# The last part of a convolution and attention kernel: other units ahead of the last stage, x's half of the fusion first, output stores on ScalarE's queue, a one-image unit last

## The chip, the cores and the metric

One core of one Trainium2 chip runs the kernel. The metric is the device time of one execution in microseconds; the figure for a kernel is the median of its runs. One further execution was recorded by the hardware profiler; its span and its own time are given below. Engines are named as the profile names them: PE multiplies matrices (PEld is its weight load), ACT is the scalar engine, DVE the vector engine, POOL GpSimd, SP the sync engine; ACTq, SPq and POOLq are rows of DMA issues of these engines.

## The reference

Two images of 256 channels and 64 x 64 pixels go through two layers.

Layer 0 is attention over all pixels, fused with its input:

```python
q = proj(Wq, bq) / math.sqrt(hd); k = proj(Wk, bk); v = proj(Wv, bv)     # 8 heads of 32
attn = softmax(einsum('bnd,bmd->bnm', q, k))                             # 4096 x 4096 a head
fuse = einsum('bnm,bmd->bnd', attn, v)
hybrid = conv1x1(concatenate([x, fuse], axis=1), Wf, bf)
x = hybrid * m + x * (1.0 - m)
```

Layer 1 is a channel gate, attention inside windows of 8 x 8 pixels, and a gate out of two grouped convolutions:

```python
x = x * sigmoid(relu(xp @ ca_w1 + ca_b1) @ ca_w2 + ca_b2)
o = softmax(q k / sqrt(64)) v                  # 4 heads in each of 64 windows, then @ out_w
x = shuffle(x + o)                             # channels in 4 groups
y = relu(bn1(conv7x7(x, sa_w1, groups=64)))
y = bn2(conv7x7(y, sa_w2, groups=64))
return x * sigmoid(y)
```

All is in float32. The convolutions need rows of the whole image with a border of three, so a channel's convolution can begin only when every part of that image has been through layer 1's attention.

## The kernel before, in words

**Main loop.** `pipeline` walks through 1024 slots: two images b, eight chunks c of 512 pixels, two groups g of four heads, 32 blocks m of 128 keys. Each slot makes scores on PE (L580), exponentials on ACT (L590), the product with v on PE (L609) and the running sum of the exponentials on DVE (L611). `products` also registers, by `at(delay, action)`, what follows the last block of a chunk: the sums of the exponentials (`denominators`, L632), their reciprocal, two spreads of it over channels (`spread`, L647, with a copy on ACT) and the product that makes `f` (L664). A counter `now` runs with the slots, and an action is done when its delay has passed.

**Stage.** After each chunk a generator `stage(b, c)` is put in the queue `stages`. Between its `yield`s it records the fusion of x and f (eight matmuls, L677; x is kept in `xw`, and the first two of four products for an output half are of x, the others of f), the channel gate (L706, L714, a second small matmul and a tanh, L729), the projections of the windows' attention (L748, L761), scores, exponentials, v, a transpose, the product (L876, L887), the output projection (L898, L906), the sum (L909), and four stores (L924) of the result to `xs` in DRAM, two on SP and two on POOL. In the main loop a stage goes on by one step every four slots. After the last slot comes the stage of the last chunk of image 1, with no attention work left beside it: this is where the change lies.

**Convolutions.** `convolve` is another generator. Its work is cut into `items`: a unit `u` is 4 of the 64 convolution groups (16 channels), for image 0, image 1 or both. The two 7 x 7 convolutions are matmuls with banded weights, read as `w_s[u]` (896 KB, L959). For an item, x is read from DRAM (`load_x`, L966, 420 KB an image), the first convolution is 56 matmuls (L987) with a relu on ACT (L995), the second 56 matmuls (L1011) with two tanh (L1021) and a scaling copy (L1027) on ACT, the gate product on DVE (L1033), and 12 stores an image to the output (L1039), of which SP issues half and POOL half. The recorded order is: first convolution of item k+1, second convolution of item k, gate and stores of item k, loads. The first convolution has one PSUM buffer, the second three pairs, and the output tile `z` two buffers.

`items` lists 9 units of image 0, then the same 9 of image 1, then 7 units of both images: 25 items. Units of image 0 can run while the last chunk of image 1 is still in its stage, and fill its waits: after the last slot the loop below records, by turns, a step of the stage and a step of `convolve`. `now` goes on by 2 a turn.

```python
while later or stages:
    now[0] += 2
    run_later()
    run_stages()
    if later or stages:
        next(conv)
staged.append(True)
```

Only after `staged` is set may x of image 1 be loaded, since the last stage writes it. The four early x tiles `xea` come from before; later x tiles `xla` take over buffers of the attention.

**What sets the order.** The order of instructions on each engine is the order of recording, and each engine goes through its own list in order. A DMA that an engine issues stands in that list, too. An instruction waits on semaphores of what it depends on. DMAs of SP and ACT report their end in eight shared completion counters in turn, and a DMA waits until the one before it on its counter has landed.

Of the kernel before, what the change touches and what calls it, by code (L numbers as in the profile page):

```python
# [10 lines left out]
F32 = mybir.dt.float32  # L11
# [6 lines left out]
B, C, H, W = 2, 256, 64, 64  # L18
N = H * W
P = 128  # L20
KC = C // P
CH = 512
# [3 lines left out]
HG = 4  # L26
# [2 lines left out]
NPIECE = NMB // PB  # L29
AHEAD = 2  # L30
EB = 8
EARLY = 1 + EB
HEADS1, HD1 = 4, 64
WS = 8
NW = W // WS
# [2 lines left out]
WP = W + 2 * PAD  # L38
# [5 lines left out]
UG = 4  # L44
UQ = UG // 4
NU = NG // UG
# [8 lines left out]
def conv_seq_kernel(ctx: ExitStack, tc: tile.TileContext, a, out):  # L55
    nc = tc.nc
# [129 lines left out]
    with (  # L186
# [9 lines left out]
        for n in ("bq", "bk"):  # L196
            t = w0.tile([P, KC], F32, name=n)
            for g in range(KC):
                for j in range(HG):
                    h = HG * g + j  # L200
# [209 lines left out]
    def spread(row, n):  # L410
        f = row.shape[-1]
        return row.rearrange("p u f -> u p f").to_broadcast([NU, n, f])
# [58 lines left out]
    def pipeline(arm, shifted, pools):  # L471
# [25 lines left out]
        def at(delay, action):  # L497
            later.append((now[0] + delay, action))
# [99 lines left out]
        def products(i):  # L598
            b, c, g, m = slots[i]
            if m == 0:  # L600
                acc[0] = avp.tile([P, CH], F32, tag="av", name=f"av{arm}_{i}")
                acc[1] = ep.tile([P, HG, CH], F32, tag="sum", name=f"sum{arm}_{i}", bufs=3)
                totals[b, c, g] = acc[1]
            av, total = acc[0], acc[1]
            e, v = es[i], vts[b, c, g, m // PB]
            start, stop = m == 0, m == NMB - 1
            for j in range(HG):
                r = slice(32 * j, 32 * j + 32)
                nc.tensor.matmul(av[r, :], v[:, m % PB, r], e[:, j, :], start=start, stop=stop)  # L609
            if m > 0:  # L610
                nc.vector.tensor_add(total, first[0] if m == 1 else total, e)  # L611
            e = es.pop(i)
            if start:
                first[0] = e
            if stop:
                if g == 0:
                    fts[b, c] = fp.tile([P, KC, CH], F32, tag="f", name=f"f{arm}_{b}_{c}")
                f = fts[b, c]
                nc.scalar.copy(f[:, g, :], av)  # L619
                if g == 0:  # L620
                    return
                both = [totals.pop((b, c, gg)) for gg in range(KC)]
                inv = fp.tile([P, P], F32, tag="inv", name=f"inv{arm}_{i}")
                rd = fp.tile([P, KC, 4, P], F32, tag="rd", name=f"rd{arm}_{i}")


                def denominators():
                    s = psum2(f"dn{arm}_{i}")
                    for h in range(HEADS0):
                        for q in range(4):  # L630
                            r = slice(32 * q, 32 * q + 32)
                            nc.tensor.matmul(  # L632
                                s[r, 0, 0:P],
                                keysum[:, h].rearrange("p i h -> p (i h)"),
                                both[h // HG][:, h % HG, q * P : (q + 1) * P],
                                start=(h == 0),
                                stop=(h == HEADS0 - 1),
                            )
                    nc.scalar.copy(inv, s[:, 0, 0:P])


                def spread(hh):
                    t = psum2(f"rd{arm}_{i}_{hh}")
                    for gg in range(KC):
                        for q in range(2):
                            r = slice(64 * hh + 32 * q, 64 * hh + 32 * q + 32)
                            nc.tensor.matmul(  # L647
                                t[:, q, gg * P : gg * P + P],
                                spread_h[r, gg].rearrange("p j d -> p (j d)"),
                                inv[r, :],  # L650
                                start=True,
                                stop=True,
                            )
                    nc.scalar.copy(
                        rd[:, :, 2 * hh : 2 * hh + 2, :],
                        t[:, :, 0 : KC * P].rearrange("p q (g n) -> p g q n", g=KC),
                    )


                at(8, denominators)  # L660
                at(9, lambda: nc.vector.reciprocal(inv, inv))
                at(10, lambda: spread(0))
                at(11, lambda: spread(1))
                at(12, lambda: nc.vector.tensor_mul(f, f, rd.rearrange("p g q n -> p g (q n)")))  # L664


        def stage(b, c):
# [4 lines left out]
            t = gp.tile([P, KC, CH], F32, tag="t", name=f"t{tag}")  # L672
            x1 = gp.tile([P, KC, CH], F32, tag="x1", name=f"x1{tag}")
            xw = [x[:, kc, :].rearrange("p (r w c) -> p w r c", r=WS, w=NW) for kc in range(KC)]
            for oc in range(KC):
                for kc in range(2 * KC):
                    nc.tensor.matmul(  # L677
                        s[:, oc, :],
                        wf[:, kc, oc * P : (oc + 1) * P],
                        xw[kc] if kc < KC else f[:, kc - KC, :],  # L680
                        start=(kc == 0),
                        stop=(kc == 2 * KC - 1),
                    )
            for oc in range(KC):
                nc.scalar.activation(  # L685
                    t[:, oc, :], s[:, oc, :], AF.Identity, bias=bf[:, oc : oc + 1]
# [9 lines left out]
            nxt = (b, c + 1) if c + 1 < NCHUNK else (b + 1, 0)  # L696
            if nxt[0] < B:
                load_x(*nxt)
            yield

            half = CH // 2
            toks = [slice(half * h, half * h + half) for h in range(2)]
# [33 lines left out]

            u = wp.tile([P, KC, CH], F32, tag="u", name=f"u{tag}")
            nc.vector.scalar_tensor_tensor(u, t, 1.0, x1, ALU.add, ALU.mult)  # L738
            yield

            qks, es_, mxs, sums = [], [], [], []

# [72 lines left out]
                nc.vector.tensor_mul(e, e, rs.unsqueeze(2).to_broadcast([P, 8, 64]))  # L815

            project_out(0, project(0))
            yield
            window_scores(0)
            yield  # L820

            s = project(1)
            window_exp(0)
            project_out(1, s)
            yield
            window_scores(1)
            normalise(0)
            yield
# [34 lines left out]
                                )  # L863
            pt = wp.tile([P, 2, 2, KC, 2, 64], F32, tag="pt", name=f"pt{tag}")
            nc.scalar.copy(pt, st)
            yield

            s = psum2(f"o{tag}")
            o = s.rearrange("p w (a t q) -> p w a t q", a=KC, t=4)
# [14 lines left out]
            for kc in range(KC):  # L884
# [5 lines left out]
                    AF.Identity,  # L890
                    bias=bqkv[:, 4 + kc : 5 + kc],
                )
            yield
            s = psum2(f"op{tag}")
            y = gp.tile([P, KC, CH], F32, tag="t", name=f"y{tag}")
            for oc in range(KC):
# [32 lines left out]

        items = [(u, (b,)) for b in range(B) for u in range(EARLY)]
        items += [(u, tuple(range(B))) for u in range(EARLY, NU)]
        staged = []

        def convolve():
# [34 lines left out]
            def load_rows(k):  # L971

                while len(xs) < min(k + 1, len(items)) and (
                    staged or B - 1 not in items[len(xs)][1]
                ):
                    load_x(len(xs))
# [53 lines left out]
            def gate(k, z):  # L1030
                u, images = items[k]
                x = xs[k][:, 0 : nb * len(images), :, PAD : PAD + W]
                nc.vector.tensor_mul(z, z, x.rearrange("p n g x -> p g n x"))  # L1033
                for m, b in enumerate(images):
                    for n, (x0, r0, r1) in enumerate(BLOCKS):
                        for i in range(4):
                            p = 32 * i + 1 - x0
                            eng = nc.sync if i >= 2 else nc.gpsimd
                            eng.dma_start(  # L1039
                                dst[b, i, r0:r1, UG * u : UG * u + UG, :],  # L1040
                                z[p + r0 : p + r1, :, nb * m + n, :],
                            )


            load_rows(3)
# [5 lines left out]
            yield  # L1051
            for k, (u, images) in enumerate(items):
                while len(xs) <= k + 1 < len(items):
                    if staged:

                        for n in range(3):
                            t = ep.tile([P, HG, CH], F32, tag="sum", name=f"xl{arm}{n}", bufs=3)
                            t = t.rearrange("p h n -> p (h n)")[:, 0 : B * nb * UG * WP]
                            xcs.append(
                                t.rearrange("p (n g w) -> p n g w", n=B * nb, g=UG, w=WP)  # L1060
                            )
                        xcs.append(pool.tile([P, B * nb, UG, WP], F32, name=f"xl{arm}3"))
                        load_rows(k + 4)
                    else:
                        yield
                conv1(k + 1)
                yield
                z = conv2(k)
                yield
                gate(k, z)  # L1070
                if xcs or k + 4 < EARLY:
                    load_rows(k + 4)
                if B - 1 in images and u:
                    load_w(u + EB)
# [8 lines left out]

        def run_stages():
            while stages:
                if next(stages[0], stages) is not stages:
                    return
                stages.popleft()

        banded = bands()  # L1090
# [6 lines left out]
        for i, (b, c, g, m) in enumerate(slots):  # L1097
# [12 lines left out]
            if rest:  # L1110
                rest()
            if g == KC - 1 and m == NMB - 1:
                at(13, lambda b=b, c=c: stages.append(stage(b, c)))
            run_later()
            if i % 6 == 1:
                next(banded, None)
# [3 lines left out]
        att.close()  # L1120
        psum_layout(f"conv{arm}", 3, 1)
        conv.send(att.enter_context(tc.tile_pool(name=f"late{arm}", bufs=1)))
        while later or stages:
            now[0] += 2
            run_later()
            run_stages()
            if later or stages:
                next(conv)
        staged.append(True)
        for _ in conv:  # L1130
# [86 lines left out]
```

## Time and profile before

| | |
|---|---|
| runs | 3069.12, 3069.18, 3074.34 us; median 3069.18 |
| profiled execution, its own time | 3070.01 us |
| its span in the profile | 3068.2 us |
| mean granted PE clock | 0.989 |
| PE busy | 2988.2 us, 97% |
| DVE busy | 2516.5 us, 82% |
| ACT busy | 2450.6 us, 80% |
| POOL busy | 344.7 us, 11% |
| last attention product ends | about 2821.8 us |
| from there to the end of the span | 246.4 us |

Times of the timeline count from the start of the span. The shares are means over the whole span, and some nine tenths of it is the main loop; the part that the change reorders is the last 246 us. Busy time of an engine leaves out DMA issues of ACT and SP, which the profile shows in rows of their own (ACTq, SPq), though they hold the engine's list just as well.

### The profile page before, as it was taken

What the parts mean: (1) busy time and instruction counts of PE and PEld (TensorE: products, weight loads), DVE (VectorE), ACT (ScalarE), POOL (GpSimd) and SP (SyncE); (2) the same over time, 40 slices, a digit from 0 to 9 for tenths busy, and PEclk for the clock granted to TensorE, in tenths of its full rate; (3) what the DMA queues carried; (4) which work ended last, traced back from release to release, by engine and by line L of the source; (5) the groups of instructions that cost most, each with busy time, mean ns of one, the idle gap of its engine ahead of it and who ended that gap; (6) DMA issues with size and microseconds to landing.
All of it is one profiled execution on the core that took longest, in us unless ns stands there. A gap on an engine that the chain in (4) does not pass through costs nothing.

```text
span 3068.2 us, 61291 instructions
## 1 busy us (share of the span) xinstructions
PE 2988.2 (97%) x25338; PEld 1015.0 (33%) x25338; DVE 2516.5 (82%) x1398; ACT 2450.6 (80%) x4122; POOL 344.7 (11%) x591
## 2 busy tenths in 40 slices
PE   8989989999999999999999999999999999999897
PEld 4442222232222222222232222323232223224675
DVE  3229989999999999998999999999999998988211
ACT  2239879898989898998989898989898988987423
POOL 7110000001010101010101001010101010000346
PEclk9989999999999999999999999999999999999998
DMA  6953112314141413242322214132413242314264
GB/s 197 356 162 76 59 50 64 67 63 72 59 81 60 75 64 69 66 75 68 66 66 61 66 59 73 59 74 61 78 60 68 70 71 66 109 57 134 61 203 97
DMA packets 160352, 264.20 MB, mean 86 GB/s; under 512 B 43944, under 2 KB 62620, under 8 KB 160064
## 3 DMA queue, kind: packets, MB, share of 16 engines
q1 hardware_dynamic: 133664, 221.72, 24.4%
q0 software_dynamic: 22432, 35.91, 8.4%
q8 instruction: 201, 3.29, 0.4%
q10 hardware_dynamic: 3968, 2.57, 0.3%
q14 instruction: 87, 0.71, 0.1%
HBM read 197.89 MB, written 65.21 MB: 86 GB/s over the span
## 4 chain that ended last, share of the span: by engine, by line
PE 70%; DVE 16%; issue 2%; DMA 2%; ACT 2%; POOL 1%; SPq 0%; DVEq 0%; ACTq 0%; POOLq 0%
PE sa L580 28%; PE ava L609 26%; DVE suma L611 15%; PE qka L748 4%; PE hya L677 4%; PE vwa L834 2%; PE c2a L1011 1%; POOL out_dram L1039 1%; PE c1a L987 1%; ACT ea L590 1%; PE opa L898 1%; DMA out_dram<-za 1%; PE sca L782 1%; PE rda L647 1%; PE pta L857 1%
## 5 line engine op out<-in xcount | busy, mean ns | idle before, releaser
L611 DVE TENSOR_TENSOR suma<-suma,ea 128x2048 f32<-128x2048 f32 x960 | 2198.7, 2290 | 86.0 <-ACT ea L590 1.8
L590 ACT ACTIVATE ea<-sa 128x512 f32<-128x512 f32 (+1 forms) x3072 | 2044.2, 745 | 85.0 <-PE sa L580 36.9
L580 PE MATMUL sa<-qa,ka 32*128 32x512 f32 x8192 | 1189.9, 641 | 8.2 <-DMA ka<-ks 8.0
L609 PE MATMUL ava<-ea,va 128*32 128x512 f32 x8192 | 1092.3, 605 | 0.3 <-ACT fa L619 0.3
L580 PEld LDWEIGHTS sa<-qa,ka 32*128 32x128 f32 x8192 | 333.1, 183 | 762.8 <-ACT ea L590 688.6
L609 PEld LDWEIGHTS ava<-ea,va 128*32 128x32 f32 x8192 | 161.6, 108 | 780.6 <-issue 754.3
L924 POOL DMA_DIRECT2D xs<-xo x94 | 65.9, 708 | 2353.5 <-DVE xo L909 2353.4
L1039 POOL DMA_DIRECT2D out_dram<-za x192 | 108.0, 571 | 128.1 <-DVE za L1033 92.4
L748 PE MATMUL qka<-ua,qkv_w 128*128 128x512 f32 x256 | 118.4, 605 | 0.7 <-DVE ua L738 0.7
L1033 DVE TENSOR_TENSOR za<-za,xla 128x768 f32<-128x768 f32 (+1 forms) x16 | 20.9, 1309 | 101.4 <-ACT za L1027 65.0
L1011 PE MATMUL c2a<-yca,wa 32*128 32x192 f32 (+1 forms) x1400 | 100.0, 427 | 0.3 <-ACT za L1021 0.3
L685 ACT ACTIVATE ta<-hya,bf 128x512 f32<-128x512 f32 x32 | 20.2, 684 | 96.9 <-PE hya L677 96.9
L1011 PEld LDWEIGHTS c2a<-yca,wa 32*128 32x128 f32 x1400 | 91.8, 316 | 10.9 <-issue 9.7
L689 DVE TENSOR_TENSOR ta<-ta,mca 128x512 f32<-128x512 f32 x32 | 22.0, 689 | 88.0 <-ACT ta L685 88.0
L1021 ACT ACTIVATE za<-c2a 128x384 f32<-128x384 f32 (+1 forms) x50 | 26.3, 578 | 79.7 <-DMA out_dram<-za 47.9
L803 ACT ACTIVATE ewa<-ewa,mxwa 128x64 f32<-128x64 f32 x256 | 85.5, 362 | 0.0
L611 DVE TENSOR_TENSOR suma<-ea,ea 128x2048 f32<-128x2048 f32 x32 | 73.1, 2286 | 15.0 <-DMA va<-vs 15.0
L231 ACT ACTIVATE qsq<-q,bq 128x512 f32<-128x512 f32 x32 | 22.0, 687 | 74.1 <-DVE qst L230 72.6
L430 POOL DMA_DIRECT2D ws<-r2s x112 | 69.5, 623 | 68.5 <-DMA xs<-xo 33.2
L761 ACT ACTIVATE qka<-qka,qkv_b 128x512 f32<-128x512 f32 x64 | 40.7, 694 | 44.2 <-PE qka L748 44.2
L987 PE MATMUL c1a<-xla,wa 128*32 128x192 f32 (+1 forms) x896 | 58.7, 413 | 14.2 <-DMA xla<-xs 14.2
L230 DVE TENSOR_SCALAR qst<-q,bq 128x512 f32<-128x512 f32 x32 | 24.0, 751 | 59.1 <-PE q L219 41.2
(139 smaller groups left out, 1674.7 us busy)
## 6 DMA issues: line engine op xcount, KB each, us to landing
ka<-ks SPq DMA_DIRECT2D x256, 256.0 KB
va<-vs SPq DMA_DIRECT2D x256, 256.0 KB
ws<-zero POOLq DMA_DIRECT2D x16, 896.0 KB, 17.1
wa<-ws SPq DMA_DIRECT2D x16, 896.0 KB
xs<-xo POOLq DMA_DIRECT2D x78, 140.0 KB, 7.2
xla<-xs SPq DMA_DIRECT2D x23, 420.0 KB
x<-in_x_dram SPq DMA_DIRECT2D x16, 512.0 KB
ks<-kst SPq DMA_DIRECT2D x32, 256.0 KB
```

What stands on the lines that cost most here:

```text
L430: nc.gpsimd.dma_start(band2[:, at0 : at0 + step * (n - 1) + 1 : step, :], spread(r2_s[k : k + 1, :, i], n),)
L580: nc.tensor.matmul(heads[j], k[r, cols], q[r, g, :], start=True, stop=not shifted)
L590: nc.scalar.activation(e[:, h, :], tile, AF.Exp, scale=SCALE0)
L609: nc.tensor.matmul(av[r, :], v[:, m % PB, r], e[:, j, :], start=start, stop=stop)
L611: nc.vector.tensor_add(total, first[0] if m == 1 else total, e)
L677: nc.tensor.matmul(s[:, oc, :], wf[:, kc, oc * P : (oc + 1) * P], xw[kc] if kc < KC else f[:, kc - KC, :], start=(kc == 0), stop=(kc == 2 ...
L748: nc.tensor.matmul(s[:, j, :], wqkv[:, kc, o : o + P], u[:, kc, :], start=(kc == 0), stop=(kc == KC - 1),)
L803: nc.scalar.activation(e[:, n, :], e[:, n, :], AF.Exp, bias=mx[:, n : n + 1], accum_out=rs[:, n : n + 1],)
L924: eng.dma_start(x_s[b, n, p + r0 : p + r1].rearrange("r g w -> g r w"), xo[64 * h : 64 * h + 64, oc, r0 - WS * c : r1 - WS * c, :],)
L987: nc.tensor.matmul(s[32 * j : 32 * j + 32, 0 : n * W], w[:, j, d, :], xs[k][:, 0:n, j, d : d + W], start=(d == 0), stop=(d == KS - 1),)
L1011: nc.tensor.matmul(tiles[j // 2][:, j % 2, 0 : n * W], w[r, d], y[r, 0:n, d : d + W], start=(d == 0), stop=(d == KS - 1),)
L1039: eng.dma_start(dst[b, i, r0:r1, UG * u : UG * u + UG, :], z[p + r0 : p + r1, :, nb * m + n, :],)
```

## The change

1. `items`: 7 units of image 0 alone (`EARLY` 7), units 1 to 6 of image 1 alone, units 7 to 15 of both images, and unit 0 of image 1 last: 23 items.
2. The loop after the last slot: `now` goes on by 1 a turn. One step of `convolve` is recorded ahead of it, and one when `now` reaches the delay `DN` (8), so the first two first convolutions stand ahead of the denominators. While the stage runs, a step of `convolve` follows only where the stage yields `True`, which marks places where its next step waits for another engine; other yields go straight on.
3. The fusion makes x's products for both output halves first, then f's.
4. Output stores: all items but the last two divide their stores between POOL and ACT; the last but one between POOL, ACT and SP; the last between SP and ACT. SP otherwise issues loads, and two of the stage's stores to `xs`.
5. The late x tiles are set up, and loads up to item `EARLY + 3` recorded, at the first step of `convolve` after the stage's end (`more`), also between a second convolution and its gate.
6. The delays 8 to 13 are written as `DN` and so on, with the same values.

On PE, the first and second convolutions that stand ahead of the end of the last stage's output projection are now 5 and 4; they were 9 and 8.

```diff
-EARLY = 1 + EB
+DN = 8
+EARLY = 7
...
-            for oc in range(KC):
-                for kc in range(2 * KC):
-                    nc.tensor.matmul(
-                        s[:, oc, :],
-                        wf[:, kc, oc * P : (oc + 1) * P],
-                        xw[kc] if kc < KC else f[:, kc - KC, :],
-                        start=(kc == 0),
-                        stop=(kc == 2 * KC - 1),
-                    )
+            for half in range(2):
+                for oc in range(KC):
+                    for kc in range(KC * half, KC * half + KC):
+                        nc.tensor.matmul(
+                            s[:, oc, :],
+                            wf[:, kc, oc * P : (oc + 1) * P],
+                            f[:, kc - KC, :] if half else xw[kc],
+                            start=(kc == 0),
+                            stop=(kc == 2 * KC - 1),
+                        )
...
-            yield
+            yield True
...
-        items = [(u, (b,)) for b in range(B) for u in range(EARLY)]
-        items += [(u, tuple(range(B))) for u in range(EARLY, NU)]
+        items = [(u, (0,)) for u in range(EARLY)] + [(u, (1,)) for u in range(1, EARLY)]
+        items += [(u, (0, 1)) for u in range(EARLY, NU)] + [(0, (1,))]
...
+                if k < len(items) - 2:
+                    engines = (nc.gpsimd, nc.scalar)
+                elif k < len(items) - 1:
+                    engines = (nc.gpsimd, nc.scalar, nc.sync)
+                else:
+                    engines = (nc.sync, nc.scalar)
+                stores = 0
                 for m, b in enumerate(images):
                     for n, (x0, r0, r1) in enumerate(BLOCKS):
                         for i in range(4):
                             p = 32 * i + 1 - x0
-                            eng = nc.sync if i >= 2 else nc.gpsimd
-                            eng.dma_start(
+                            stores += 1
+                            engines[stores % len(engines)].dma_start(
                                 dst[b, i, r0:r1, UG * u : UG * u + UG, :],
                                 z[p + r0 : p + r1, :, nb * m + n, :],
                             )
+            def more():
+                if staged and not xcs:
+                    for n in range(3):
+                        t = ep.tile([P, HG, CH], F32, tag="sum", name=f"xl{arm}{n}", bufs=3)
...
+                    load_rows(EARLY + 3)
+                return bool(xcs)
...
                 while len(xs) <= k + 1 < len(items):
-                    if staged:
...
-                        load_rows(k + 4)
-                    else:
+                    if not more():
                         yield
                 conv1(k + 1)
                 yield
+                more()
                 z = conv2(k)
                 yield
+                more()
                 gate(k, z)
...
         def run_stages():
             while stages:
-                if next(stages[0], stages) is not stages:
-                    return
+                waits = next(stages[0], stages)
+                if waits is not stages:
+                    return waits
                 stages.popleft()
...
-        while later or stages:
-            now[0] += 2
+        next(conv)
+        while later:
+            now[0] += 1
             run_later()
-            run_stages()
-            if later or stages:
+            if now[0] == len(slots) + DN:
+                next(conv)
+        while stages:
+            if run_stages():
                 next(conv)
```

More of the change, by code (lines that the diff above doesn't have):

```diff
@@ L657, in spread @@
                     )
[L660 to L664, printed above, removed]
+                at(DN, denominators)
+                at(DN + 1, lambda: nc.vector.reciprocal(inv, inv))
+                at(DN + 2, lambda: spread(0))
+                at(DN + 3, lambda: spread(1))
+                at(DN + 4, lambda: nc.vector.tensor_mul(f, f, rd.rearrange("p g q n -> p g (q n)")))
         def stage(b, c):
@@ L738, in stage @@
             nc.vector.scalar_tensor_tensor(u, t, 1.0, x1, ALU.add, ALU.mult)
-            yield
+            yield True
             qks, es_, mxs, sums = [], [], [], []
@@ L817, in stage @@
             project_out(0, project(0))
-            yield
+            yield True
             window_scores(0)
@@ L824, in stage @@
             project_out(1, s)
-            yield
+            yield True
             window_scores(1)
@@ L865, in stage @@
             nc.scalar.copy(pt, st)
-            yield
+            yield True
             s = psum2(f"o{tag}")
@@ L892, in stage @@
                 )
-            yield
+            yield True
             s = psum2(f"op{tag}")
@@ L1042, in gate @@
                             )
+            def more():
+                if staged and not xcs:
+                    for n in range(3):
+                        t = ep.tile([P, HG, CH], F32, tag="sum", name=f"xl{arm}{n}", bufs=3)
+                        t = t.rearrange("p h n -> p (h n)")[:, 0 : B * nb * UG * WP]
+                        xcs.append(t.rearrange("p (n g w) -> p n g w", n=B * nb, g=UG, w=WP))
+                    xcs.append(pool.tile([P, B * nb, UG, WP], F32, name=f"xl{arm}3"))
+                    load_rows(EARLY + 3)
+                return bool(xcs)
             load_rows(3)
@@ L1053, in convolve @@
                 while len(xs) <= k + 1 < len(items):
-                    if staged:
[L1056 to L1062, printed above, removed]
-                        load_rows(k + 4)
-                    else:
+                    if not more():
                         yield
@@ L1112, in pipeline @@
             if g == KC - 1 and m == NMB - 1:
-                at(13, lambda b=b, c=c: stages.append(stage(b, c)))
+                at(DN + 5, lambda b=b, c=c: stages.append(stage(b, c)))
             run_later()
```

## The prediction

> **What bounds the kernel now.** I read the windows first, because the change concerns only what follows the last attention product at about 2821.8 us (columns: stretch, its length, busy us and instructions of PE, PEld, DVE, ACT and POOL, clock, DMA share, GB/s).
>
> ```profile
> 2850.00:2900.00 50.00, 48.74 (x738) 37.35 (x740) 11.51 (x16) 22.68 (x62) 16.82 (x30) 1.00 0.24 53
> 2900.00:2950.00 50.00, 35.60 (x616) 28.83 (x616) 6.09 (x7) 13.14 (x24) 15.97 (x29) 0.86 0.40 101
> 2950.00:3000.00 50.00, 48.86 (x768) 38.71 (x768) 7.51 (x7) 16.45 (x28) 22.64 (x41) 1.00 0.82 248
> ```
>
> PE fills every stretch except 2900–2950, where it loses 14 us and some clock. The timeline (start, duration, engine and line; in brackets the idle time before and its releaser) shows where.
>
> ```profile
> 2903.05 3.70 PE L898 MATMUL opa<-ota,out_w 128*128 128x512 f32 x8 [1.33 <-ACT ota L887]
> ...
> 2908.50 1.43 POOL L924 DMA_DIRECT2D xs<-xo  x2 [1.42 <-DVE xo L909]
> ...
> 2916.30 1.99 SPq L966 DMA_DIRECT2D xla<-xs  x4
> ...
> 2919.82 4.71 PE L987 MATMUL c1a<-xla,wa 128*32 128x192 f32 x56 [13.07 <-DMA xla<-xs]
> ```
>
> The last stage ends with its projection at 2906.75, writes x to DRAM, reads it back, and PE idles 13.07 us; the convolution after it takes 4.71 us instead of 2.5. Next, the period of a two-image unit, again from the timeline:
>
> ```profile
> 3004.59 1.51 ACT L1021 ACTIVATE za<-c2a 128x768 f32<-128x768 f32 x2 [4.27 <-DMA out_dram<-za]
> ...
> 3006.14 1.49 ACT L1027 ACTIVATE za<-za 128x1536 f32<-128x1536 f32 x1
> ...
> 3007.66 1.76 DVE L1033 TENSOR_TENSOR za<-za,xla 128x1536 f32<-128x1536 f32 x1 [7.88 <-ACT za L1027]
> ...
> 3009.44 5.05 SPq L1039 DMA_DIRECT2D out_dram<-za  x12
> 3009.71 6.73 POOL L1039 DMA_DIRECT2D out_dram<-za  x12 [2.92 <-DVE za L1033]
> ...
> 3014.24 1.51 ACT L1021 ACTIVATE za<-c2a 128x768 f32<-128x768 f32 x2 [4.28 <-DMA out_dram<-za]
> ```
>
> Tanh to tanh is 9.65 us, which is PE's work (4.8 + 4.9). ACT works 3.6 us of it; the stores lie on SP and POOL. The end is POOL's last 24 stores, to 3061.68, then 6.5 us of landing and closing:
>
> ```profile
> 3048.23 13.45 POOL L1039 DMA_DIRECT2D out_dram<-za  x24 [2.87 <-DVE za L1033]
> ```
>
> ACT issues DMAs only at the kernel's start; these are the price for the change's stores:
>
> ```profile
> 25.00 0.45 ACTq L108 DMA_DIRECT2D out_w<-in_out_w_dram  x1
> ...
> 26.14 0.35 ACTq L108 DMA_DIRECT2D out_b<-in_out_b_dram  x1
> ```
>
> **What the Trainium skill says.** "PSUM — Partial Sum Buffer", section "Engine vs sequencer instructions": ScalarE's queue is strict FIFO. So a store on ACT holds up the relu and tanh behind it; no tail row of before shows this. "Perfetto Trace Analysis", section "DMA Instruction — HWDGE": the profile's time of an issue includes a wait for a generator that the issuing sequencers share. At 0.75 us SP and ACT issue together, 0.49 and 0.50 us each, against 0.35 to 0.45 above. "DMA: Bandwidth & Descriptors", section "Issuing engines are not separate DMA queues": a second issuer saves sequencer time alone. The trace agrees that this is what is paid: 12 stores hold SP 5.05 us. "TensorE: Matmul & The Clock Gate", section "What's actually happening": after an idle window of about 3.4 us the clock is halved. The 4.71 us convolution agrees.
>
> **The change part by part.** Times are of the profiled execution (span 3068.2; it took 3070.01, the runs' median 3069.18, so span plus 1.0).
>
> Units: 18 singles at 5.97 us and 7 doubles at 9.65 (175.0) become 14 and 9 (170.4), 4.6 less PE work; it is contained in the next two sums.
>
> 1. *The stage comes earlier.* Before, 9 first and 8 second convolutions stand on PE ahead of the end of the projection; in the changed order 5 and 4. Four of each leave: 4 x 2.5 + 4 x 3.55 = 24.2 us. Against that, PE gains a wait: ACT's order is now six stores of unit 0, a relu, then the gate's sigmoid, so PE's second small projection waits for ACT (2845.8 + six stores 2.5 + relu and sigmoid 1.0 = 2849.3, PE being done at 2845.5): 3.7. So −20.5: the projection ends at 2886.2. If the clock falls in that gap, +2 at most.
> 2. *The round trip.* 13.07 us from projection to the first convolution that needs it: 2899.3. Under it now stand two units of 6.05, so PE waits about 1 and the clock stays. Before, that convolution began at 2919.82 and lost 2.2 to the clock. If this cover were gone, 12 us return.
> 3. *PE work from there.* One second convolution 3.55, seven singles (six and the last) at 5.97 = 41.8, nine doubles 86.85: 132.2, to 3031.5. The same sum for before, 3.55 + 9 x 5.97 + 7 x 9.65 + 2.2 = 127.0, gives 3046.8; the trace has 3048.9, so the method lacks 2.
> 4. *Stores on ACT.* SP's issues took 0.42 (5.05/12), ACT's loads 0.33 to 0.60; I take 0.42. Single: tanh to store 2.77, six stores 2.5, relu 0.45, launch gaps 0.1 = 5.85, just under 5.97, so hidden. Double: tanh to stores 4.85, twelve stores 5.05, relu 0.6 = 10.5 against 9.65: ACT becomes the bound, and the next tanh, and through PSUM the next second convolution, are late by 0.9. Eight such periods: +7.2. At 0.33 it is nothing; at 0.50 it is +15.
> 5. *Load queue and waits.* SP holds loads alone, so they issue earlier: worth nothing while PE is full. But in the built order the stores of units 10 to 14 also wait on ACT until an x or W load sharing their completion counter has landed. Two x loads and a W are 1.74 MB, at the 234 to 316 GB/s of this phase 5.5 to 7.4 us: up to 1.4 over a single's period, nothing over a double's. Three singles make 4, including the 2 lacking in step 3; bounds 0 and 9.
> 6. *The end.* Last second convolution ends 3031.5 + 7.2 + 4 = 3042.7, the one before at 3039.2. From there ACT and DVE 4.85, eight stores on ACT 3.4 (this unit is shared by three queues), the single's tanh, copy and product 2.77, six stores 2.5, landing and close 6.5: 20.0. Before, from the same point (3043.0) it was 25.2; the gain is smaller last stores.
> 7. *x's half of the fusion first.* In 15 of 16 stages the eight matmuls stand in the full main loop, and their waits name no f: 0, within 1 either way. In the last, 4 x matmuls fill the wait for f; step 1 holds it. DN only names the 8.
>
> Sum: 3039.2 + 20.0 = 3059.2 of span, 3060.2 for the runs, 0.3% faster.
>
> **Rivals.** *PE stays the bound:* an ACT issue of at most 0.35 us hides behind PE. For: the 0.33 and 0.35 rows. Against: stores of 24 KB took SP 0.42. Then 3031.5 + 2 − 3.55 + 4.85 + 2.8 + 2.77 + 2.1 + 6.5 = 3049, with 1.0 3050.
> *ACT becomes a bound that eats all (slower):* at 0.53 us an issue, because ACT's stores and SP's loads wait for each other as at 0.75 us, or stores took SP over a microsecond as they did near 2955. Single 6.5 instead of 5.97 (12 times, +6), double 11.9 (+18), waits 4, end +1.5: 3031.5 + 28 − 3.55 + 21.5 = 3077.5, with 1.0 3078.5. It decides from 0.47 to 0.48 us upward. Against: most SP issues were 0.38 to 0.43.
> *The stage does not come earlier as laid out:* ACT's stores also stand between the stage's own steps (scores, exponentials, copies), and each may expose 2.5 us of PE as in step 1; four would cost 10: 3070, no change. For: PE already waits 1.33 on ACT ahead of the projection, in the second fence.
>
> **How the numbers follow.** 0.2% (6 us) is what a measurement of this kernel can tell from no change: faster means under 3063, slower over 3075.3. As laid out 0.48 (3053 to 3067, a quarter of it above 3063), PE-bound 0.23 (3044 to 3053), stage held up 0.15 (3065 to 3073), ACT eats all 0.14 (3074 to 3085, a tenth of it below 3075.3). Faster 0.36 + 0.23 = 0.59; slower 0.13; same 0.12 + 0.15 + 0.01 = 0.28. I predict 3060; the range 3046 to 3076 leaves out the ends of the outer cases; for a faster result alone it is 3046 to 3063.
>
> **What would show it.** Step 1: projection L898 ends near 2886, one PE gap near 3.7 before the sigmoid's projection. Step 2: first convolution from xla near 2899, with clock 1.00. Step 4: ACTq L1039 rows of x6 and x12 at 2.5 and 5.0 us, tanh to tanh 10.5 in doubles, PE idle 0.9 in each. Step 5: periods over 7 us at units 10 to 12. Step 6: 20 us from the last double's end. Wrong if an ACT store takes under 0.35 or over 0.47 us, if PE gaps in the stage exceed 8, or if the main loop's end moves from 2821.8.

## The result, and the profile after

The changed kernel takes 3082.98 us (median of 20 runs, 3073.83 to 3091.84); the kernel before took 3070.05 in the runs beside it (20 runs). The ratio is 1.0037, 95% interval 1.0027 to 1.0047: slower, where 0.3% faster was predicted.

The profiled execution took 3089.66 us with a span of 3087.9, so it lies 6.7 above its median. About 3.6 of its distance to the profile of before is no effect of the change: the main loop is 3.5 us later already at 1518 us and stays so, while the first run below, with the same main loop, begins its tail at 2821.55, as before. The other 3 us or so lie in this execution's tail. I therefore compare tails, from the start of the first tail convolution (L987 before, L991 after) to the end of the span: 246.7 us before (2821.49 to 3068.2), 262.8 after (2825.12 to 3087.9).

In the lines, xea and xla are the early and the later x, wa the weights, c1a and c2a the results of the first and second convolution, yca the relu's output and za the output tile. The windows of the changed kernel (columns as in the prediction: stretch, length, busy us and instructions of PE, PEld, DVE, ACT, POOL, clock, DMA share, GB/s):

```profile
2850.00:2900.00 50.00, 43.60 (x632) 31.49 (x628) 11.54 (x17) 22.10 (x61) 10.21 (x18) 0.90 0.18 44
2900.00:2950.00 50.00, 46.08 (x832) 41.08 (x836) 7.00 (x8) 14.62 (x28) 27.30 (x49) 0.97 0.65 179
2950.00:3000.00 50.00, 44.00 (x484) 27.42 (x484) 5.44 (x4) 13.57 (x19) 21.38 (x38) 0.90 0.61 193
```

The hole of 14 us at 2900–2950 is nearly closed, as it should be. But PE now has holes in the other two stretches, which it filled before, and the clock falls there too. The table of waits of the tail says behind what (who waits for whom: us in total, times, longest):

```profile
ACT yca L999 <- DMA out_dram<-za: 117.2, 19, 9.9
...
PE c1a L991 <- ACT yca L999: 18.1, 11, 4.0
```

Nineteen relus of ACT wait for output stores. A relu needs no store; it stands behind ACT's issues in ACT's list. One period of a two-image unit in the timeline:

```profile
2975.50 1.76 DVE L1037 TENSOR_TENSOR za<-za,xla 128x1536 f32<-128x1536 f32 x1 [9.96 <-ACT za L1031]
2977.08 4.96 PE L1015 MATMUL c2a<-yca,wa 32*128 32x384 f32 x56
...
2977.28 0.91 SPq L970 DMA_DIRECT2D xla<-xs  x2
2977.29 8.07 ACTq L1050 DMA_DIRECT2D out_dram<-za  x12
...
2985.41 0.59 ACT L999 ACTIVATE yca<-c1a,cbias 128x384 f32<-128x384 f32 x1 [9.95 <-DMA out_dram<-za]
2985.89 1.50 ACT L1025 ACTIVATE za<-c2a 128x768 f32<-128x768 f32 x2
2986.05 7.51 PE L991 MATMUL c1a<-xla,wa 128*32 128x384 f32 x56 [4.02 <-ACT yca L999]
```

Twelve issues hold ACT 8.07 us, from 2977.29 to 2985.36; the relu starts 0.05 later, and only then can PE begin its next first convolution, 4.02 us idle and at half clock (7.51 instead of 4.82). From tanh to tanh the first eight periods of two-image units are 13.46, 12.59, 12.77, 12.16, 12.10, 11.55, 10.54 and 10.36 us, together 95.5; at PE's 9.65 they would be 77.2.

The stage and the round trip in the same timeline:

```profile
2853.83 2.77 ACTq L1050 DMA_DIRECT2D out_dram<-za  x6
...
2857.49 2.08 PE L723 MATMUL ca2a<-ga,ca_w 64*128 64x256 f32 x8 [3.89 <-ACT ga L717]
...
2893.67 3.70 PE L901 MATMUL opa<-ota,out_w 128*128 128x512 f32 x8
...
2913.39 2.53 PE L991 MATMUL c1a<-xla,wa 128*32 128x192 f32 x56 [0.80 <-ACT yca L999]
```

The wait of 3.89 us before the gate's second matmul is the one foreseen. The projection ends at 2897.4, and PE waits 0.80 for the first unit with a later x, instead of 13.07.

### The profile page after: what moved, and what is told of

Its sections match the earlier page's. It is cut to its first block, busy times and chain, and to the rows that moved or that the text cites. A ratio compares the mean times of both kernels' runs of the same rounds, so it can differ in the third digit from the quotient of the medians.

```text
span 3087.9 us, 60751 instructions
## 1 busy us (share of the span) xinstructions
PE 3001.1 (97%) x25114; PEld 1010.7 (33%) x25114; DVE 2516.0 (81%) x1396; ACT 2448.4 (79%) x4114; POOL 339.1 (11%) x581
## 4 chain that ended last, share of the span: by engine, by line
PE 78%; DVE 8%; ACT 2%; DMA 2%; issue 1%; POOL 1%; ACTq 0%; DVEq 0%
PE sa L581 32%; PE ava L610 30%; DVE suma L612 7%; PE qka L751 4%; PE hya L680 4%; DMA out_dram<-za 2%; PE vwa L837 2%; PE opa L901 2%; POOL out_dram L1050 1%; PE c2a L1015 1%; ACT ea L591 1%; DVE za L1037 1%; ACT za L1025 1%; PE rda L648 1%; ACT za L1031 1%
## 5 line engine op out<-in xcount | busy, mean ns | idle before, releaser
L1037 DVE TENSOR_TENSOR za<-za,xla 128x1536 f32<-128x1536 f32 (+1 forms) x16 | 22.5, 1409 | 136.3 <-ACT za L1031 136.3
L999 ACT ACTIVATE yca<-c1a,cbias 128x192 f32<-128x192 f32 (+1 forms) x23 | 11.2, 486 | 127.9 <-DMA out_dram<-za 117.2
L991 PE MATMUL c1a<-xla,wa 128*32 128x384 f32 (+1 forms) x896 | 68.8, 460 | 15.7 <-ACT yca L999 15.6
```

The source lines that it names most:

```text
L991: nc.tensor.matmul(s[32 * j : 32 * j + 32, 0 : n * W], w[:, j, d, :], xs[k][:, 0:n, j, d : d + W], start=(d == 0), stop=(d == KS - 1),)
```

## The experiments

In the profiles of these runs the tail begins anywhere from 2816.5 to 2826.3 us, so small steps are read from the tails; but a tail is one execution, and a step of a few us that the medians do not confirm is not shown. Theory A: ACT's store issues make ACT the bound. Rival B: the new order of units and stage, with the falling clock, costs the time. Rival C: with stores back on SP the loads come late. Ratios are to the kernel before, run beside them.

**SP in ACT's place.**

```diff
-                    engines = (nc.gpsimd, nc.scalar)
+                    engines = (nc.gpsimd, nc.sync)
```

> The changed kernel, with SP in ACT's place for the stores of all items but the last two. Theory A (ACT's store issues, 5.1 to 8.1 us for twelve, make ACT the bound of the units): two-image periods of 9.65 to 9.8 instead of 10.4 to 13.5, ACT never waiting behind stores in the stage, last second convolution about 25 us earlier than in the changed kernel; 3055 to 3062 us, 0.3 to 0.5% faster than before. Rival B (the new order of units and stage, with the clock falling in the new PE gaps, is what costs): 3075 to 3085, about as the changed kernel. Rival C (loads queue behind stores on SP and arrive late): periods over 10.5 with PE waiting for xla or wa, 3065 to 3075.

Measured: 3054.03 us, ratio 0.9953 [0.9937, 0.9970]; tail 230.75. One line of the change is worth 29 us by the medians, a little more than expected. Two periods of the timeline:

```profile
2956.66 1.51 ACT L1025 ACTIVATE za<-c2a 128x768 f32<-128x768 f32 x2 [4.28 <-DMA out_dram<-za]
...
2966.27 1.51 ACT L1025 ACTIVATE za<-c2a 128x768 f32<-128x768 f32 x2 [4.26 <-DMA out_dram<-za]
...
2971.12 5.98 SPq L1050 DMA_DIRECT2D out_dram<-za  x12
```

9.61 us, PE's pace, though SP takes 5.03 to 6.47 us for its twelve issues: on SP nothing of the path stands behind them. A holds; B and C fall. The rest of the change makes the kernel faster than before by 0.47%. One place is left, in the timeline of this run:

```profile
2893.92 2.00 SPq L970 DMA_DIRECT2D xla<-xs  x4
...
2896.05 24.25 SPq L1050 DMA_DIRECT2D out_dram<-za  x30
...
2903.71 0.87 ACT L1025 ACTIVATE za<-c2a 128x384 f32<-128x384 f32 x2 [9.53 <-DMA out_dram<-za]
2904.25 4.25 PE L1015 MATMUL c2a<-yca,wa 32*128 32x192 f32 x52 [3.69 <-ACT za L1025]
```

Stores of items 3 and 4 stand on SP behind loads that wait for the stage's result; item 5's tanh waits 9.53 us for an output tile, and PE 3.69.

**Three queues.** `(nc.gpsimd, nc.scalar, nc.sync)` in that line.

> The changed kernel with POOL, ACT and SP sharing the stores of all items but the last two, 4 each for one image and 8 each for two. Theory A: ACT in a two-image unit 4.85 + 8 issues + 0.6: 8.9 at 0.43 us an issue, 9.9 at the 0.56 that the changed kernel showed while loads flow: periods 9.65 to 10.2, 3056 to 3066 us. Rival B: 3075 to 3085. If the waits of ACT's issues, not their number, set the cost, periods stay over 11.

Measured: 3071.96 us, 1.0012 [1.0005, 1.0019]; 11 us faster than the changed kernel, and no gain on before. Fewer issues help, but the size was missed: while loads flow, eight issues took ACT 5.8 to 5.9 us (first pair below), so the first two periods are 11.2 to 11.3, as the last sentence of the expectation has it; later 3.6 to 3.8 (second pair), with periods of 9.6 to 9.9.

```profile
2982.56 6.52 SPq L1050 DMA_DIRECT2D out_dram<-za  x8
2982.57 5.92 ACTq L1050 DMA_DIRECT2D out_dram<-za  x8
...
3014.97 3.58 SPq L1050 DMA_DIRECT2D out_dram<-za  x8
3014.97 3.79 ACTq L1050 DMA_DIRECT2D out_dram<-za  x8
```

SP and ACT issue at the same moment in both pairs, at 0.74 to 0.82 us an issue, pauses included, in the first and 0.45 to 0.47 in the second. So their sharing alone does not make the rows long.

**ACT in the kernel before.**

```diff
-                            eng = nc.sync if i >= 2 else nc.gpsimd
+                            eng = nc.scalar if i >= 2 else nc.gpsimd
```

> The kernel before with ACT in SP's place for all output stores, and nothing else changed. Theory A: two-image periods 9.65 become 10.4 to 13, 7 of them: +10 to +18; one-image units while loads flow +0.5 each, and stage steps behind stores some us: 3084 to 3098 us, 0.5 to 0.9% slower than before. Rival B: within 5 us of before.

Measured: 3086.11 us, 1.0062 [1.0039, 1.0085]; tail 262.7 instead of 246.7. ACT's stores cost about 17 us without anything else of the change. In its timeline the relu again stands behind the stores:

```profile
3013.31 5.98 ACTq L1039 DMA_DIRECT2D out_dram<-za  x12
...
3019.34 0.59 ACT L995 ACTIVATE yca<-c1a,cbias 128x384 f32<-128x384 f32 x1 [7.86 <-DMA out_dram<-za]
```

**The fusion's order alone.** The kernel before with the fusion loop of the change.

> The kernel before with x's products first in the fusion, and nothing else. In the main loop nothing (the two traces run in parallel from 700 us on); in the last stage at most 2 us either way: 0.9985 to 1.001 of before. Rival: if the half clock of the last fusion in the changed kernel (8 matmuls of x in 6.3 us instead of 3.9) comes from the order itself, it shows here too, and the fusion ends later than 7.1 us after its start.

Measured: 3068.47 us, 0.9999 [0.9990, 1.0007]: nothing. Its last fusion ran at full clock. The half clock in the changed kernel's profile (eight x matmuls in 6.33 us instead of 3.70) is therefore not the order's alone: of the nine other runs with the changed stage only the one with ACT's stores in the two-image units shows it, in part (5.4 us).

**Which units lose.** ACT's stores only in the seven units around the stage (`nc.scalar if k < EARLY else nc.sync`), or only in the two-image units (`nc.scalar if len(items[k][1]) > 1 else nc.sync`).

> The changed kernel, with ACT's stores only in the seven units of image 0 that lie around the last stage, SP's from item 7 on. It gives the stage's share of the loss alone. In the changed kernel's trace the stage and the round trip reach the eighth first convolution of a later x tile 7 us later than with SP's stores (94.2 against 86.9 us after the first convolution of the tail); two-image periods should be 9.65 again: 3059 to 3063 us. Rival: the loss in the stage is taken up by waits that follow anyway, 3053 to 3057.

> The changed kernel, with ACT's stores only in the nine two-image units (the last but one stays shared by three), SP's before. It gives the doubles' share: eight periods sum to 95.5 us in the changed kernel against 77.2 at PE's pace, so up to 18 us over the run with SP's stores: 3066 to 3073 us, with periods of 11.5 to 13.5 while loads flow and 10.4 after. If ACT's issues were long only because of what the stage and the one-image units left behind, periods near 10.4 throughout: 3058 to 3061.

Measured: 3055.73 us, 0.9956 [0.9942, 0.9969], for the first; 3075.84, 1.0022 [1.0012, 1.0033], for the second. Over the run with SP's stores that is +1.7 and +21.8 of the 29.0 (by the tails +1.5 and +21.7). The remaining 5.4 are left for the one-image items 7 to 12, whose tanh-to-tanh sum is 46.7 us in the changed kernel and 42.2 with SP's stores. The rival of the first expectation was right: the stage's loss from ACT is about as large as SP's own blocked stores there. The doubles' loss was foreseen as up to 18. Their eight periods took 95.1 us, as in the changed kernel, but with SP's stores they take 74.8 and not the 77.2 set against them, since in the last (7.36) PE has only a one-image first convolution to do; that makes 20.3. The eight batches took 52.3 us, the first of them the longest:

```profile
2964.28 9.41 ACTq L1050 DMA_DIRECT2D out_dram<-za  x12
2973.74 0.59 ACT L999 ACTIVATE yca<-c1a,cbias 128x384 f32<-128x384 f32 x1 [11.29 <-DMA out_dram<-za]
```

**Why the issues are long.** In the first run late weights and x are not loaded again, but earlier tiles used, which changes part of the computation; in the second, the late loads go to POOL.

```diff
+                if u > EB + 1:
+                    ws[u] = ws[u - EB]
+                    return
...
+                if k > EARLY + 9:
+                    xs[k] = xcs[k % 4]
+                    return
```

```diff
-                nc.sync.dma_start(t, w_s[u])
+                (nc.gpsimd if u > EB else nc.sync).dma_start(t, w_s[u])
...
-                    nc.sync.dma_start(
+                    (nc.gpsimd if k > EARLY + 3 else nc.sync).dma_start(
```

> The changed kernel without the weight loads of units 10 to 15 (it uses earlier units' weights) and without the x loads of the last six items (it uses x tiles that are there): part of the computation is thereby changed. If the flow of loads makes ACT's issues long, the twelve issues of every two-image unit take 5.0 to 5.3 us, as the last ones of the changed kernel do, the periods 10.4 to 10.7, and it ends 8 to 12 us earlier than the changed kernel. If the issues are long by themselves, they stay at 6.7 to 8.

> The changed kernel with the late x and weight loads on POOL instead of SP: the same bytes, but no longer in the completion counters that ACT's and SP's DMAs share. If ACT's stores wait for a load on their counter, twelve issues take 5.0 to 5.4 us here; if the transfers in flight slow the issues down whoever started them, 6 to 8 us stay. The time itself decides nothing, since POOL issues slowly and loads may come late.

Without loads: 3068.13 us, 0.9998 [0.9989, 1.0007], 15 us under the changed kernel; six of its eight batches take 5.13 to 5.24 us, but two 6.25 and 6.53. With loads on POOL: 3073.49, 1.0012 [1.0006, 1.0019]; batches of 5.74, 7.11, 5.97, 6.15, then 5.22 to 5.11. From the timeline of the first and of the second:

```profile
2962.29 5.14 ACTq L1056 DMA_DIRECT2D out_dram<-za  x12
2967.48 0.58 ACT L1005 ACTIVATE yca<-c1a,cbias 128x384 f32<-128x384 f32 x1 [7.01 <-DMA out_dram<-za]
```

```profile
2977.55 7.11 ACTq L1050 DMA_DIRECT2D out_dram<-za  x12
2984.71 0.59 ACT L999 ACTIVATE yca<-c1a,cbias 128x384 f32<-128x384 f32 x1 [8.98 <-DMA out_dram<-za]
```

Sums of the eight batches are 51.1 us in the changed kernel, 45.6 with loads on POOL, 43.7 without; eight undisturbed ones of 5.13 would be 41.0. Issue by issue, the traces show two different things in what is above that. The first is in the batch of 8.07 us of the changed kernel (shortest, median and longest of its issues, in ns):

```profile
L1050 ACTq DMA_DIRECT2D out_dram<-za x12: 310/388/442, 2977.3 to 2985.0; - x12
```

No issue is long there; ACT stands still between issues three times, for 0.55 to 1.66 us. In nine of the eleven such pauses in the eight batches, the DMA before on the store's completion counter is an x load that SP issued together with the batch, as at 2977.28; in two it is a store of ACT. The pauses come to 6.7 us in the changed kernel, 1.9 with the loads on POOL and 0.3 without loads. So loads on the shared counters make most of the excess.

The second is single issues of over 0.5 us. What they take above 0.45 us comes to 3.1 us, 2.4 and 2.3 in the three runs, so loads are not their cause. One from the batch of 6.25 us of the run without loads, and from what the DMA engines moved during that batch:

```profile
2984.51 1.46 ACTq L1056 DMA_DIRECT2D out_dram<-za  x1
...
q8 instruction: 1, 0.02, 0.9%
```

A fetch of instructions (packets that the profile calls instruction) ran at the time of each of the twelve such issues in these three runs, and no batch without a fetch has one. No run changes the fetches, so that they are the cause is not shown. The gain of 15 us without loads exceeds the foreseen 8 to 12; how much of it lies in the one-image units was not measured.

**The last unit.** SP's stores, with the items as 7 units of image 0, 7 of image 1, 9 of both.

> As the run with SP in ACT's place, but unit 0 of image 1 stands with the other one-image units, and a two-image unit is last (its stores 12 on SP and 12 on ACT). Theory: from the end of the last but one second convolution to the span's end it is a double's work, tanh to store 4.85 instead of 2.77 and 12 issues instead of 6: +3 to +6, 3056 to 3061. Rival: the last but one item is a double in both, its stores fill the same queues, and the end is the same within 1.5.

Measured: 3057.38 us, 0.9963 [0.9949, 0.9977]; tail 234.75 instead of 230.75. By the tails the one-image unit at the end is worth the 4 us foreseen, by the medians 3.3; the intervals of the two ratios overlap.

**A version that beats both.** First only items 3 and 4 on ACT; then, besides, the last but one unit on POOL and SP.

```diff
-                    engines = (nc.gpsimd, nc.scalar)
+                    engines = (nc.gpsimd, nc.scalar if k in (3, 4) else nc.sync)
                 elif k < len(items) - 1:
-                    engines = (nc.gpsimd, nc.scalar, nc.sync)
+                    engines = (nc.gpsimd, nc.sync)
```

> As the run with SP in ACT's place, but items 3 and 4 leave half their stores to ACT: these are the two whose stores stood on SP behind loads that wait for the stage's result, so that tanh of item 5 waited 9.5 us for an output tile and PE 3.7. Theory D (the only good of ACT's stores lies there): PE's gap of 3.7 and the slow convolution after it go, 4 to 6 us under that run, 3047 to 3051. Rival: the two times six issues on ACT (2.5 us each) stand ahead of the stage's own steps and give back what they save: 3052 to 3056.

> SP in ACT's place but for items 3 and 4, and the last but one unit on POOL and SP alone, so that the last unit's tanh does not stand behind eight issues on ACT (5.4 us in the run before, tanh 8.0 us after the one before it ended). The last tanh then waits for the output tile of the double before, about 4 us earlier: 2 to 4 us under the run with items 3 and 4 on ACT by the tail's length, 3049 to 3053 us. Rival: SP's twelve stores then end later than what they replace, and the end is the same within 1.

Measured: 3055.17 us, 0.9946 [0.9932, 0.9960], for items 3 and 4 alone; 3050.75, 0.9940 [0.9926, 0.9953], for both. The tails are 230.75 with SP's stores, 227.6 and 226.8. By the tail the first step is worth 3.2 us, less than expected, but its median lies in its rival's range, 1.1 us above that of the run with SP's stores, so a gain is not shown. ACT took 4.52 and 3.68 us for the six issues that were put at 2.5, and PE still idles 2.06 us behind the first of them. The second step is worth 0.8 by the tail, so its rival holds there. The last tanh does start early in its timeline, 4.47 us after the ACT work before it instead of 8.09 in the run with the first step alone,

```profile
3035.80 0.87 ACT L1025 ACTIVATE za<-c2a 128x384 f32<-128x384 f32 x2 [4.47 <-DMA out_dram<-za]
...
3038.57 4.10 ACTq L1050 DMA_DIRECT2D out_dram<-za  x6
```

but the last six issues then take 4.10 us instead of 2.87. The version with both edits is 0.6% faster than the kernel before, and 1% faster than the changed one.

## Why the prediction was wrong

The prediction put the tail at 3059.2 − 2821.8 = 237.4 us; the profile has 262.8. The 25.4 us divide by its own steps:

- **Step 1, the stage.** The projection was put 64.4 us after the tail's start, 60.7 without ACT's wait; it ended at 72.2, and at 63.7 with SP's stores, so that some 3 us were missed whoever stores (1.35 of them PE's wait ahead of the spread). ACT's wait before the gate was foreseen at 3.7 and measured at 3.89. The clock's price in that gap, "+2 at most", held: 1.0 for the matmul after the gate and 0.6 for the convolution behind it. But the clock fell at two more places, for which nothing was put down: the fusion lost 2.5 and another convolution 1.5. With ACT's stores in the first seven units alone, the same order up to here, the projection ended at 67.1, so some 5 us of the 7.8 are that execution's.
- **Step 2, the round trip.** The cover works, the 13.07 us of idle PE are gone. From the projection's end it took 16.0 us instead of 13.1, and what PE waited for at its end was not x but a relu behind six stores of 5.03 us.
- **Step 3, PE's work.** Right: with SP's stores the doubles run at 9.6 us.
- **Step 4, the failed step, with step 5's wait in doubles.** Step 4 named the mechanism, ACT becoming the bound of two-image units, and took 0.42 us an issue from SP's 5.05 us batch. The eight batches took 51.1 us, 0.53 each, and the periods 95.5 instead of 8 x 10.55 = 84.4: 11 us more. The price of an undisturbed issue was right (0.43 on ACT). Missing were the 6.7 us of pauses on shared counters, a wait that step 5 knew but put at "nothing over a double's" period, and the 3.1 us of single long issues. The 5.05 batch had neither; the one just before it in the kernel before had a long one, and so had some of before's rows of 6 issues, in 3.0 to 3.8 us while loads flow. These were set against the price in a rival instead of taken into it.

```profile
2999.80 6.13 SPq L1039 DMA_DIRECT2D out_dram<-za  x12
```

- **Step 5, waits on loads.** Put at 4 for three one-image units; items 7 to 12 lost 4.6 to SP's stores by their periods. A period over 7 us without a double in it was seen at one of the units named, 7.95. From the first later x to the last convolution, steps 3 to 5 together were 16.4 short.
- **Step 6, the end.** From the last second convolution to the end 14.7 us, predicted 16.5: right within 2.
- **Step 7.** Nothing, as said; the run with it alone shows it.

To rounding, 25.4 is 7.8 + 2.9 + 16.4 − 1.8, of steps 1, 2, 3 to 5, and 6. Of the prediction's signs of being wrong, an ACT store over 0.47 us came true. The rival that ended slower was the right one: at 0.53 us an issue it gave 3078.5, and the median is 3083. Both its reasons are seen, since stores and loads did wait for each other, through the counters, and some issues took over a microsecond. That the mean is just its 0.53 is luck, as the batches range from 0.43 to 0.67. It had 0.14. "PE stays the bound" fell with the same rows; "the stage is held up" costs 1.7 us in the runs over SP's stores, which lose time there too.

The Trainium skill's sentence on ACT's queue ("PSUM — Partial Sum Buffer", section "Engine vs sequencer instructions": strict FIFO) is what the traces show in every double: the relu starts 0.05 us after the twelfth issue. The halved clock after an idle window ("TensorE: Matmul & The Clock Gate", section "What's actually happening") shows as first convolutions of 6.5 to 7.5 us. The page names an idle window of about 3.4 us; here idle times of 1.86 to 3.18 us were already followed by half clock, and the measurement decides. It costs little here, since ACT, not PE, ends last: after the one of 7.51 us, ACT's tanh waited 0.39.

## What to carry to other kernels

Twelve store issues held ACT's list for 5.1 to 8.1 us here, longer than the relu, tanh and copy of the unit together; put stores on a queue behind which nothing of the critical path stands, and move to a compute engine only those that a blocked queue would hold back. Price a batch of issues with the waits between them, from a row of the same load phase and not from a quiet one, and look for loads that leave at the same moment on the same completion counters. If the price decides the sign, give the case beyond the threshold its weight. When a change of several parts loses, look for the part that can be undone alone: here one line hid a gain of 0.5%.

## What the hardware showed that was not expected

Undisturbed, twelve stores were issued in 5.13 to 5.15 us on ACT (0.43 each) and in 5.03 to 5.05 on SP, and two engines at once still issued eight each at 0.45 to 0.47. Rows of 6.7 to 8.1 us are made longer by two things that a row does not tell apart: pauses of up to 1.66 us until the DMA before on a shared counter has landed, and single issues of up to 1.85 us, each at the time of an instruction fetch, on SP too (1.47 us in the batch of 6.13).

PE fell to half clock after an idle time of 1.86 us in the changed kernel (3.76 us for a one-image first convolution instead of 2.54) and kept the full clock after 2.36 us in the run with ACT's stores in the kernel before (4.82 us for a two-image one). So the length of the gap alone does not decide; what does was not tested.

```profile
2905.20 3.76 PE L991 MATMUL c1a<-xea,wa 128*32 128x192 f32 x56 [1.86 <-ACT yca L999]
```

```profile
3008.62 4.82 PE L987 MATMUL c1a<-xla,wa 128*32 128x384 f32 x56 [2.36 <-ACT yca L995]
```
